# Gated cross-attention with a mixture of experts: the first query group's statistics in pairs in a written order, two products without sums first, raw key blocks read from the input

## The chip, the cores and the metric

The kernel runs on one core of one Trainium2 chip. The metric is the device time of one execution in microseconds; the median of several runs is compared. All data is float32.

## The reference

One decoder layer on 4096 tokens `x` of width 512, with a context `ctx` of 3202 rows of width 512. What matters here is the first half; `ln` is a layer norm without scale or offset.

```python
q    = ln(x)                                     # 4096 x 512
Sim  = (q @ w1)[:, None] + (ctx @ w2)[None, :] + (q * w3) @ ctx.T + b_sim
A    = softmax(Sim, axis=1)
hat  = A @ ctx                                   # 4096 x 512
Batt = softmax(max(Sim, axis=1))
bar  = Batt @ q                                  # one row
x    = x + tanh(g_xattn) * (concat[q, hat, q*hat, q*bar] @ W_qv + b_qv)
# then ln, a router over 8 experts, top 2, capacity 1280, two-layer GELU experts, scaled sum
x    = x + tanh(g_ffn) * moe(ln(x))
```

## The kernel before

The tokens are worked on in 8 groups of 512 (`g` = 0 to 7). For each group the kernel computes the scores (`stage_s`), their exponentials (`stage_e`), the weighted values (`stage_v`) and a dense product; after the last group come routing and the experts. Scores stand with context rows in partitions and tokens along the free dimension.

**The scores.** The 3202 context rows are two halves of 12 tiles of 128, one tile more, and two single rows. A key tile `j` joins tile `j` of both halves, transposed, and is worked on in pairs: six pairs a group. The 512 x 512 block of such a pair (two halves of rows, two halves of tokens, two halves of the 512 features) is computed by a Strassen-Winograd scheme: seven products of half size in place of eight, from sums of key blocks (`S1`, `S2`, `S4`, and a difference in the place of `A21`; on DVE, in `build`) and sums of query blocks (`T1`, `T2`, `T4`, and a difference in the place of `B12`; on DVE, in `right_sums`). The function `chain` issues them in the order 1, 6, 7, 5, 2, 4, 3 and joins their results on DVE (`u2`, `u3` and four sums, the score tile `E`); products 1 and 2 are summed in one PSUM bank, as are 5 and 3. Product 1 is raw keys `A11` times raw queries `B11`, product 2 is `A12` times `B21`; the others need at least one sum. One product is 8 matmul records of 128 x 256 in the profile (`pas`, `p6s`, `p7s`, `pbs`, `p4s` at L512).

**The key tiles.** In group 0, `build(j)` loads the four raw blocks of a tile from the input `ctxt_t` (512 KB, SP's queue, L361), computes the four sums (L364 to L368), and after the pair's products ACT's queue writes all seven blocks to the scratch tensor `kt_d[j]` (896 KB, L520). In groups 1 to 7 `load_keys` reads the seven blocks back (896 KB, SP's queue, L432). These tiles, and the value tiles, share a pool of five buffers (`st`), so a load waits until PE has done with the tile that had the buffer, and in group 0 also until it has been written to `kt_d`.

**The first group's queries** (`stage_a_first`) can't be prepared beside earlier work. Four tiles of 128 tokens are loaded by SP (L202). `layernorm` works tile by tile: DVE computes statistics and aggregates them (L93, L95), POOL raises the variance to the power -0.5 (L99, L100, and L101 for its square root, `sd`), DVE normalises (L102). PE transposes (L110), ACT copies from PSUM to `qT` (L205), and after each second tile the queries are scaled and shifted to `Qp` (L212 on DVE, L214 on ACT). Hints (`tc.issue_after`) order part of this: tile `t`'s statistics come after the normalising of tile `t`-2. Otherwise a planner puts each engine's instructions in order before the run; on the chip each engine follows its order and waits on semaphores.

**Constants.** ACT's queue first loads seven small constants (L57 to L165), computes `tanh` of the two gates (L69, L70; ACT loads its function table just before), and later the larger `wv` and `bqv` and the store of `qT` (L219 to L225). The column means of the router's weights `wrc` are subtracted in `stage_a_rest`, written after the third pair; the planner puts the matmuls for it (`wrps`, L253) between product 1 and product 6 of the first pair.

**Counters.** The transfers of SP's and ACT's queues share eight completion counters in turn. A transfer whose counter still belongs to an earlier transfer waits for that one to land, and what is queued behind it on its engine waits too.

Of the kernel before, what the change touches and what calls it, by code (L numbers as in the profile page):

```python
# [14 lines left out]
P = 128  # L15
# [5 lines left out]
def gated_layer(ctx, tc, x, x_t, ctxt, ctxt_t, ctxt_c, ctxt_r, g_xattn, g_ffn, w_sim, w_sim_r, b_sim, W_qv, W_qv_t, b_qv, b_qv_c, w_router, b_router, w1, b1, w2, b2, out):  # L21
# [35 lines left out]
    nc.scalar.dma_start(ws, w_sim)  # L57
# [4 lines left out]
    nc.scalar.dma_start(bsim, b_sim.partition_broadcast(P))  # L62
    gx = const.tile([P, 1], F32, name="gx")
    nc.scalar.dma_start(gx, g_xattn.partition_broadcast(P))
    gf = const.tile([P, 1], F32, name="gf")
    nc.scalar.dma_start(gf, g_ffn.partition_broadcast(P))
    bqv = const.tile([P, D], F32, name="bqv")
    tgx, tgf = gx, gf
    nc.scalar.activation(tgx, gx, AF.Tanh)  # L69
    nc.scalar.activation(tgf, gf, AF.Tanh)  # L70
# [13 lines left out]
    nc.scalar.dma_start(wrc, w_router.rearrange("(c p) e -> p c e", p=P))  # L84
    we = const.tile([P, 4, DC, E], F32, name="we")
    sd = const.tile([P, NT], F32, name="sd")

    scales, normed = [], []

    def layernorm(sm, dst, src, t):  # L90
        st = sm.tile([P, 6], F32, name=f"st{t}", tag="st")
        with tc.issue_after(normed[-2]) if len(normed) > 1 else ExitStack():
            nc.vector.bn_stats(st, src)  # L93
        mv = sm.tile([P, 2], F32, name=f"mv{t}", tag="mv")
        nc.vector.bn_aggr(mv, st)  # L95
        rstd = sm.tile([P, 1], F32, name=f"rstd{t}", tag="rstd")
        ve = sm.tile([P, 1], F32, name=f"ve{t}", tag="ve")
        with tc.issue_after(scales[-1]) if scales else ExitStack():
            nc.gpsimd.tensor_scalar(ve, mv[:, 1:2], EPS, None, ALU.add)  # L99
        scales.append(nc.gpsimd.tensor_tensor(rstd, ve, neghalf, ALU.pow).ins)  # L100
        nc.gpsimd.tensor_tensor(sd[:, t : t + 1], ve, rstd, ALU.mult)  # L101
        nrm = nc.vector.tensor_scalar(dst, src, mv[:, 0:1], rstd, ALU.subtract, ALU.mult)  # L102
        normed.append(nrm.ins)
        return nrm
# [19 lines left out]
    with ExitStack() as s1:  # L124
# [10 lines left out]
        kt_d = [dram.tile([P, 7, 2, P], F32, name=f"kt_d{j}", tag=f"kt_d{j}") for j in range(NJ)]  # L135

        kc_d = dram.tile([P, 4, 2, P], F32, name="kc_d", tag="kc_d")
        KSLOT = {"1": 0, "2": 1, "7": 2, "4": 3, "5": 4, "6": 5, "3": 6}
# [8 lines left out]
        nc.scalar.dma_start(bcol, b_qv_c)  # L147
# [17 lines left out]
        nc.scalar.dma_start(cr, ctxt_r)  # L165
# [19 lines left out]
        def right_sums(g, qT, Qp):  # L185

            B11, B12, B21, B22 = (Qp[:, r : r + 2, c : c + 256] for r in (0, 2) for c in (0, 256))
            T1, T2, T4 = (sb.tile([P, 2, 256], F32, name=f"q{k}_{g}", tag=f"qt{k}") for k in (1, 2, 4))
            tt(T1, B12, B11, ALU.subtract)
            t2 = tt(T2, B22, T1, ALU.subtract)  # L190
            tt(B12, B22, B12, ALU.subtract)
            tt(T4, B21, T2, ALU.subtract)
            live[g] = {"qT": qT, "t2": t2, "B": {"1": B11, "6": T2, "7": B12, "5": T1, "2": B21, "4": T4, "3": B22}}

        def stage_a_first():

            qT = sb.tile([P, DC, TG], F32, name="qT0", tag="qT", bufs=2)
            Qp = sb.tile([P, DC, TG], F32, name="Qp0", tag="Qp")
            qs = []
            for t in range(4):  # L200
                q = sb.tile([P, D], F32, name=f"q{t}", tag="q" if t < 3 else "mb", bufs=3 if t < 3 else 1)
                nc.sync.dma_start(q, x[t * P : (t + 1) * P, :])  # L202
                layernorm(sm, q, q, t)
                ps = transposed(ps_tr, q, f"qps{t}")
                cp = nc.scalar.copy(qT[:, :, t * P : (t + 1) * P], ps)  # L205
                qs.append(q)
                if t % 2:
                    h = slice((t - 1) * P, (t + 1) * P)
                    for c in range(DC):
                        w3, w2 = ws[:, 2 * DC + c : 2 * DC + c + 1], ws[:, DC + c : DC + c + 1]  # L210
                        if c < DC // 2:
                            qp = ts(Qp[:, c, h], qT[:, c, h], w3, w2, ALU.mult, ALU.add)  # L212
                        else:
                            live["qp"] = nc.scalar.activation(Qp[:, c, h], qT[:, c, h], AF.Identity, scale=w3, bias=w2)  # L214
                    if t == 1:
                        live["norm"] = qp
                if t == 2:
                    with tc.issue_after(cp.ins):
                        nc.scalar.dma_start(wv[:, 0, :], w_sim_r[:D].partition_broadcast(P))  # L219
                        nc.scalar.dma_start(  # L220
                            wv[:, 1:, :].rearrange("p r d -> p (r d)"), ctxt[L - NR :, :].flatten().partition_broadcast(P)
                        )
                        nc.scalar.dma_start(bqv, b_qv.partition_broadcast(P))
            right_sums(0, qT, Qp)
            nc.scalar.dma_start(qT_d[0], qT)  # L225
# [11 lines left out]
        def stage_a_rest(qs):  # L237
# [13 lines left out]
            ps = ps_tr.tile([P, DC, P], F32, name="wrps", tag="tr")[:, 0, :E]  # L251
            for c in range(DC):
                nc.tensor.matmul(ps, ones, wrc[:, c, :], start=c == 0, stop=c == DC - 1)  # L253
            mean = be
            ts(mean, ps, 1.0 / D, None, ALU.mult)
            tt(wrc, wrc, mean.unsqueeze(1).to_broadcast([P, DC, E]), ALU.subtract)
# [100 lines left out]

        def build(j):
# [1195 lines left out]
```

## Time and profile before

| | |
|---|---|
| median of 3 runs | 2637.51 us (2636.52 to 2645.64) |
| profiled execution | 2642.18 us, its span 2640.2 us |
| busy: PE, DVE, ACT, POOL | 2609.3, 1703.0, 462.6, 236.6 us |
| mean granted PE clock | 0.995 |
| moved | 436.07 MB, mean 165 GB/s |
| PE busy, 0 to 20 us and 20 to 40 us | 11.51 and 18.97 us |
| PE busy, each 20-us stretch from 100 to 1440 us | 20.00 us |

The profile is of one execution. Its times count from the start of the span; the execution's own time is 2.0 us longer than the span. PE is the matmul engine, PEld its weight loads, which overlap matmuls; ACTq and SPq are the engines' queues, in which they issue transfers. A row of the timeline has start, duration, engine, line, what is written and read, how many instructions, and in brackets how long the engine had been idle and what ended that. Because matmuls are pipelined, a row of eight lasts a little longer than the distance to the next one.

### The profile page before, as it was taken

Reading aid. Unit: us, or ns where it says so; the run is one execution under the profiler, and the core shown is the slowest. Engines: PE = TensorE matmul, PEld = TensorE weight load, DVE = VectorE, ACT = ScalarE, POOL = GpSimd, SP = SyncE. Lnnn points to the kernel's source line nnn. Section 1 sums busy time; section 2 is a strip of 40 time slices with the busy share of each in tenths; the row PEclk is TensorE's granted clock in tenths of the full one; section 3 lists DMA queues with packets and bytes.
Section 4 is the critical chain, followed back from the end, with each engine's and each line's share of the span. In section 5 each row is a group of like instructions: output and inputs, shape, how many; then the busy total and the mean of one; then the engine's idle time right before and its main releaser. Section 6 shows DMA issues by size and latency. Waiting matters only on the chain. (4 is left out here: it accounts for less than half of the span.)

```text
span 2640.2 us, 29718 instructions
## 1 busy us (share of the span) xinstructions
PE 2609.3 (99%) x11236; PEld 2104.7 (80%) x11236; DVE 1703.0 (65%) x3412; ACT 462.6 (18%) x796; POOL 236.6 (9%) x288
## 2 busy tenths in 40 slices
PE   8999999999999999999999998999999999999998
PEld 7748888888888888888888885777777777777776
DVE  7868856947768569478475566474757565565654
ACT  1201201201102002012020143212121111111111
POOL 0111000000001000000000155010101010101010
PEclk9999999999999999999999999999999999999999
DMA  8496656746747657467445794231324132223210
GB/s 316 150 290 234 207 180 192 244 149 179 255 158 196 220 162 239 159 189 245 153 144 203 279 351 162 79 124 64 128 72 145 71 128 88 104 92 100 76 60 20
DMA packets 182959, 436.07 MB, mean 165 GB/s; under 512 B 17454, under 2 KB 84270, under 8 KB 180768
## 3 DMA queue, kind: packets, MB, share of 16 engines
q1 hardware_dynamic: 150208, 352.25, 40.4%
q0 software_dynamic: 16096, 45.04, 5.0%
q10 hardware_dynamic: 16512, 36.88, 4.0%
q8 instruction: 89, 1.46, 0.2%
q14 instruction: 54, 0.44, 0.1%
HBM read 355.71 MB, written 85.55 MB: 167 GB/s over the span
## 5 line engine op out<-in xcount | busy, mean ns | idle before, releaser
L512 PE MATMUL pas<-Qp,kt 128*128 128x256 f32 x672 | 160.5, 380 | 0.0
L1299 PE MATMUL pah<-bT,w 128*128 128x320 f32 x512 | 159.3, 433 | 0.5 <-ACT p1h L1306 0.5
L662 PE MATMUL pbv<-E,vt 128*128 128x256 f32 x672 | 147.3, 379 | 0.0
L662 PEld LDWEIGHTS pbv<-E,vt 128*128 128x128 f32 x672 | 127.7, 190 | 17.4
L512 PEld LDWEIGHTS pas<-Qp,kt 128*128 128x128 f32 x672 | 127.1, 190 | 17.4 <-ACT hqT L720 0.2
L1299 PEld LDWEIGHTS pah<-bT,w 128*128 128x128 f32 x512 | 97.0, 190 | 39.7 <-ACT p1h L1306 1.0
L602 DVE TENSOR_TENSOR E<-E,mb 128x1024 f32<-128x1024 f32 x96 | 116.2, 1226 | 11.8 <-ACT mb L589 11.8
L603 ACT ACTIVATE E<-E 128x1024 f32<-128x1024 f32 x96 | 101.0, 1058 | 129.5 <-DVE E L602 128.7
L1299 PE MATMUL pao<-w,h 128*128 128x256 f32 x512 | 120.9, 379 | 0.0
L1062 PE MATMUL x1p<-W,q2T 128*128 128x264 f32 x512 | 117.5, 391 | 0.0
L1485 POOL DMA_INDIRECT out<-acc,ti x40 | 41.1, 1027 | 851.6 <-DVE acc L1484 841.8
L1462 PE MATMUL op<-w,h 128*128 128x512 f32 x256 | 114.8, 592 | 0.0
L1299 PEld LDWEIGHTS pao<-w,h 128*128 128x128 f32 x512 | 97.3, 190 | 20.1 <-issue 7.7
L1062 PEld LDWEIGHTS x1p<-W,q2T 128*128 128x128 f32 x512 | 97.8, 192 | 16.5
L468 ACT COPY p1s<-pas 128x512 f32<-128x512 f32 x48 | 28.1, 586 | 439.1 <-issue 257.0
L538 DVE TENSOR_TENSOR M<-M,E 128x1024 f32<-128x1024 f32 x80 | 98.0, 1225 | 4.3
L693 PE MATMUL vv<-E,vc 128*128 128x512 f32 x192 | 95.2, 627 | 0.0
L1462 PEld LDWEIGHTS op<-w,h 128*128 128x128 f32 x256 | 46.6, 190 | 48.7 <-issue 43.0
L1423 DVE TENSOR_TENSOR h<-p4h,u3h 128x320 f32<-128x320 f32 x64 | 31.3, 490 | 78.0 <-PE p4h L1299 76.3
L481 ACT COPY E<-pas 128x512 f32<-128x512 f32 x48 | 28.1, 586 | 303.9 <-PE pas L512 287.6
L484 DVE TENSOR_TENSOR E<-p4s,u3s 128x512 f32<-128x512 f32 x48 | 33.1, 689 | 73.5 <-PE p4s L512 73.5
L611 DVE TENSOR_TENSOR SM<-SM,E 128x1024 f32<-128x1024 f32 x64 | 78.7, 1229 | 2.5 <-ACT E L603 2.5
(449 smaller groups left out, 5470.4 us busy)
## 6 DMA issues: line engine op xcount, KB each, us to landing
kt<-kt_d SPq DMA_DIRECT2D x84, 896.0 KB
w<-in_w SPq DMA_DIRECT2D x32, 2048.0 KB
vt<-vs_d SPq DMA_DIRECT2D x56, 768.0 KB
wp<-wt_d SPq DMA_DIRECT2D x56, 520.0 KB
kt_d<-ktb ACTq DMA_DIRECT2D x12, 896.0 KB
buf_d<-zero SPq DMA_DIRECT2D x80, 129.0 KB
xb<-buf_d SPq DMA_DIRECT2D x40, 258.0 KB
r<-r_d SPq DMA_DIRECT2D x32, 260.0 KB
```

The source lines that it names most:

```text
L484: tt(done(1, 0), p4, u3, ALU.add)
L512: nc.tensor.matmul(ps[:, jl, :], kts[j][:, KSLOT[p], k, :], B[p][:, k, :], start=start and jl == 0 and k == 0, stop=stop and k == 1, skip_ ...
L538: tt(M, M, e[:, :, h], ALU.max)
L602: live[g]["last"] = tt(e, e, m, ALU.subtract)
L603: live[g]["exp"] = nc.scalar.activation(e, e, AF.Exp)
L611: tt(SM, E_t[0][:, lr] if jj == 1 else SM, E_t[jj][:, lr], ALU.add)
L662: nc.tensor.matmul(ps[b], vt[:, j - i * JH, b * P : (b + 1) * P], right(j) if j < NJ else right_c, start=start and j == 0 and b == 0, stop ...
L693: mm = nc.tensor.matmul(ps[b], vc[:, h, b * P : (b + 1) * P], E[j // 2][:, :, h, j % 2, :] if j < NJ else ec, start=j == 0 and h == 0, sto ...
L1062: mm = nc.tensor.matmul(ps[:, j, :B1], qTs[g][:, c, q * P : (q + 1) * P], W1[:, c, j, :], start=(c == 0), stop=(c == DC - 1))
L1299: nc.tensor.matmul(ps, a, b, start=start and i == 0, stop=stop and i == len(A) - 1, skip_group_check=True)
L1462: nc.tensor.matmul(ps, hT[:, k, 2 * MH :], W2[:, k, :], start=(k == 0), stop=(k == KH - 1))
L1485: sc = nc.gpsimd.indirect_dma_start(out=out[:, :], out_offset=rows_of(ti, s), in_=acc[:, :], in_offset=None, bounds_check=N - 1, oob_is_er ...
```

## The change

- `stage_a_first`: the four loads come first in SP's queue; statistics and normalising go in a written order, two tiles' statistics and aggregations, then the next two's, then four times normalising. POOL's operations take two tiles each, `sd` all four. `in_turn` chains instructions in the given order.
- ACT starts with a `tanh` of one column of ones; the constants are loaded after it (`constants`), `wrc` first.
- PE starts with five matmuls of ones (128 x 512, results unused), then computes the sums `wrps`, ahead of the transposes.
- The query halves, the key sums of the first pair and the query sums are interleaved in a written order. The subtraction of the router's means follows them.
- The first pair's chain issues 1, 2, 6, 7, 5, 4, 3, with product 2 in a PSUM bank of its own; DVE adds it to the copied product 1 (`first`).
- The input `ctxt_t` has the second half's blocks rotated, so that the three raw blocks `A11`, `A12`, `A22` are its first six 128-column blocks. `kt_d[j]` holds only the four others (512 KB). In groups 1 to 7 `load_keys` reads three blocks from the input (384 KB) and four from `kt_d` (512 KB).
- In group 0 the writes to `kt_d` are ordered after the last copy of product 2 of the pair.

The built program of the changed kernel differs from that of before, engine by engine, up to the middle of group 0, and from then on only in the 84 key loads of SP's queue, each of which has become two.

```diff
...
-        kt_d = [dram.tile([P, 7, 2, P], F32, name=f"kt_d{j}", tag=f"kt_d{j}") for j in range(NJ)]
+        kt_d = [dram.tile([P, 4, 2, P], F32, name=f"kt_d{j}", tag=f"kt_d{j}") for j in range(NJ)]
...
-        KSLOT = {"1": 0, "2": 1, "7": 2, "4": 3, "5": 4, "6": 5, "3": 6}
+        KSLOT = {"1": 0, "2": 1, "4": 2, "7": 3, "5": 4, "6": 5, "3": 6}
...
+        def constants():
+            nc.scalar.dma_start(wrc, w_router.rearrange("(c p) e -> p c e", p=P))
+            nc.scalar.dma_start(ws, w_sim)
+            nc.scalar.dma_start(gx, g_xattn.partition_broadcast(P))
+            nc.scalar.dma_start(gf, g_ffn.partition_broadcast(P))
+            nc.scalar.activation(tgx, gx, AF.Tanh)
+            nc.scalar.activation(tgf, gf, AF.Tanh)
+            nc.scalar.dma_start(bsim, b_sim.partition_broadcast(P))
+            nc.scalar.dma_start(bcol, b_qv_c)
+            nc.scalar.dma_start(cr, ctxt_r)
...
+        def in_turn(prev, ops):
+
+            for op in ops:
+                with tc.issue_after(prev.ins) if prev is not None else ExitStack():
+                    prev = op()
+            return prev
...
+            t2 = in_turn(tt(T2, B22, T1, ALU.subtract), amid)
+            with tc.issue_after(t2.ins):
+                t3 = tt(B12, B22, B12, ALU.subtract)
+            with tc.issue_after(t3.ins):
+                t4 = tt(T4, B21, T2, ALU.subtract)
...
+            junk = sm.tile([P, 1], F32, name="junk", tag="m1")
+            with tc.issue_after(nc.scalar.activation(junk, ones[:, 0:1], AF.Tanh).ins):
+                constants()
+            warm = bank("warm").rearrange("p a b -> p (a b)")
+            for _ in range(5):
+                mm = nc.tensor.matmul(warm, ones, ones.unsqueeze(1).to_broadcast([P, 4, P]), start=True, stop=True)
+
+            wr = bank("wrps")[:, 0, :E]
+            for c in range(DC):
+                with tc.issue_after(mm.ins):
+                    mm = nc.tensor.matmul(wr, ones, wrc[:, c, :], start=c == 0, stop=c == DC - 1)
...
+            keys = [load_raw(j) for j in PAIRS[0]]
...
+            for h in (0, 2):
+                st_ = [sm.tile([P, 6], F32, name=f"st{t}", tag="st") for t in (h, h + 1)]
+                last = in_turn(
+                    last,
+                    [lambda i=i: nc.vector.bn_stats(st_[i], qs[h + i]) for i in range(2)]
+                    + [lambda i=i: nc.vector.bn_aggr(mv[:, h + i, :], st_[i]) for i in range(2)],
+                )
+                with tc.issue_after(pw.ins) if pw is not None else ExitStack():
+                    nc.gpsimd.tensor_scalar(ve[:, h : h + 2], mv[:, h : h + 2, 1], EPS, None, ALU.add)
+                pw = nc.gpsimd.tensor_tensor(
+                    rstd[:, h : h + 2], ve[:, h : h + 2], neghalf.to_broadcast([P, 2]), ALU.pow
+                )
+            nc.gpsimd.tensor_tensor(sd[:, 0:4], ve, rstd, ALU.mult)
+            last = in_turn(
+                last,
+                [lambda t=t: ts(qs[t], qs[t], mv[:, t, 0:1], rstd[:, t : t + 1], ALU.subtract, ALU.mult) for t in range(4)],
+            )
+            for t in range(4):
+                with tc.issue_after(mm.ins):
+                    ps = transposed(ps_tr, qs[t], f"qps{t}")
                 cp = nc.scalar.copy(qT[:, :, t * P : (t + 1) * P], ps)
...
+            S = [key_sums(kt) for kt in keys]
+            last = in_turn(last, [lambda c=c: queries(0, c) for c in range(DC)] + S[0][:2])
+            last = in_turn(last, [lambda c=c: queries(1, c) for c in range(DC // 2)])
+            with tc.issue_after(last.ins):
+                live["sums"] = right_sums(0, qT, Qp, S[1][:2])
+            live["sums"] = in_turn(live["sums"], S[0][3:] + S[1][3:] + S[0][2:3] + S[1][2:3])
...
+        def load_raw(j):
+            kt = st.tile([P, 7, 2, P], F32, name=f"ktb{j}", tag="st")
+            with tc.issue_after(queue[-1].ins):
+                queue.append(nc.sync.dma_start(kt[:, 0:4].rearrange("p a b w -> p (a b) w"), ctxt_t[:, j, :, :]))
+            return kt
...
-            queue.append(nc.sync.dma_start(kt, kt_d[j]))
+            nc.sync.dma_start(kt[:, :3].rearrange("p a b w -> p (a b) w"), ctxt_t[:, j, :6, :])
+            queue.append(nc.sync.dma_start(kt[:, 3:], kt_d[j]))
...
+            prod(pa, "1", True, first)
+            if first:
+                p2 = bank(f"p2{name}")
+                prod(p2, "2", True, True)
...
+            if first:
+                tt(done(0, 0), p2, p1, ALU.add)
+            else:
+                prod(pa, "2", False, True)
+                live["copied"] = nc.scalar.copy(done(0, 0), pa)
...
-                        nc.scalar.dma_start(kt_d[j], kts[j])
+                        with tc.issue_after(live.get("copied", live["qp"]).ins):
+                            nc.scalar.dma_start(kt_d[j], kts[j][:, 3:])
...
-            ctxt_t[:, j, h, :, :] = rows.T.reshape(d // P, P, -1).transpose(1, 0, 2)
+            ctxt_t[:, j, h, :, :] = np.roll(rows.T.reshape(d // P, P, -1), h * (d // P // 2), 0).transpose(1, 0, 2)
```

## Prediction, made before the changed kernel had run

> **What bounds the kernel now.** I read the engine shares first, then the timeline of the first 45 us, then windows of the clock, then the waits of SP's queue.
>
> ```profile
> PE 2609.3 (99%) x11236; PEld 2104.7 (80%) x11236; DVE 1703.0 (65%) x3412; ACT 462.6 (18%) x796; POOL 236.6 (9%) x288
> ...
> kt_d<-ktb ACTq DMA_DIRECT2D x12, 896.0 KB
> ```
>
> PE is busy for all but 31 us of the span of 2640.2. In 20-us windows it is busy 20.00 of 20.00 from 100 to 1440 us: an edit there brings nothing unless it opens a hole. What the change can gain lies in the first 45 us, where the timeline shows (start, duration, engine, what, idle before and what ended it):
>
> ```profile
> 6.16 1.12 PE L110 MATMUL qps<-ident,q 128*128 128x128 f32 x4 [6.16 <-DVE q L102]
> ...
> 10.67 2.23 PE L110 MATMUL qps<-ident,q 128*128 128x128 f32 x8 [2.04 <-DVE q L102]
> ...
> 11.12 0.55 DVE L102 TENSOR_SCALAR q<-q,mv,rstd 128x512 f32<-128x512 f32 x1 [0.60 <-POOL rstd L100]
> ...
> 12.70 3.62 PE L512 MATMUL pas<-Qp,ktb 128*128 128x256 f32 x8
> ...
> 16.11 1.40 PE L253 MATMUL wrps<-wrc,ones 128*128 128x8 f32 x8
> ...
> 17.37 1.97 PE L512 MATMUL p6s<-q,ktb 128*128 128x256 f32 x8
> ...
> 27.81 1.89 PE L512 MATMUL pas<-Qp,ktb 128*128 128x256 f32 x8
> ...
> 34.48 0.43 DVE L364 TENSOR_TENSOR ktb<-ktb 128x256 f32<-128x256 f32 x1 [4.45 <-DMA ktb<-in_ctxt_t]
> ...
> 39.36 1.99 PE L512 MATMUL pbs<-Qp,ktb 128*128 128x256 f32 x8 [1.03 <-DVE E L479]
> ```
>
> Four losses stand there. PE starts the first product at 12.70, because the last query tile is normalised only at 11.67. That product takes 3.62 us where a later one takes 1.89: its records are (3.62-0.635)/7 = 0.43 us apart, later ones (29.54-27.81)/8 = 0.216, so PE runs at half speed. The router sums (wrps) stand between products 1 and 6 and take 17.37-16.11 = 1.26. And at 39.36 PE lost 1.03 us (1.1 with the restart): a key tile landed only at 34.4, DVE stood still for it, and its later additions came late.
>
> **What the skill says.** "TensorE: Matmul & The Clock Gate", What's actually happening: the array starts at half clock and changes by how busy a free-running window of 3413 ns was. The trace agrees, though the page's clock row shows full speed in the first slices. Columns here: busy time and count per engine, then clock, DMA share, GB/s.
>
> ```profile
> 97.00:99.00 2.00, 1.76 (x12) 1.43 (x12) 1.51 (x6) 0.00 (x0) 0.28 (x1) 0.99 0.87 330
> 99.00:101.00 2.00, 2.00 (x10) 1.49 (x8) 0.55 (x1) 0.59 (x1) 0.10 (x1) 0.50 0.07 25
> 109.00:111.00 2.00, 2.00 (x9) 1.28 (x8) 2.00 (x3) 0.00 (x0) 2.00 (x1) 0.95 0.00 0
> ...
> 1631.00:1635.00 4.00, 3.25 (x15) 2.81 (x16) 0.69 (x1) 0.88 (x2) 0.00 (x0) 0.57 1.03 335
> ```
>
> The clock falls at 98.96 and rises at 109.20: 28.99 and 31.99 windows of 3.413 from the span's start. On that grid the first rise is at 17.07, in the middle of wrps, as its records show (1.40 us for eight, against 1.04 at full speed near 95 and 1.7 at half). The page's Part 4 says that transposes don't count as busy in the same way; here they do: from 1631.75 only transposes ran, and the clock rose after 3.44 us. "DMA: Bandwidth & Descriptors", Anatomy of one DMA, gives 2.0 us of fixed cost per transfer (for GpSimd's queue); I use it as an upper estimate for each additional key transfer. "Trainium Kernel Development and Optimization", Key Constraints: all queues share 16 DMA engines. The trace agrees: while ACT's kt_d writes of 896 KB drain (18 to 32 us, DMA share about 1.0), the key tile that SP issued at 27.14 took 7.3 us to land.
>
> **The change, step by step**, on the grid of this execution.
>
> *Statistics (DVE, POOL).* Tile 1 arrives at 4.77 as before, its statistics end at 5.46, two aggregations at 5.79. From an aggregation's end to the normalise it feeds before took 5.59-4.48 = 1.11 us through POOL, so pair one is ready at 6.9. But the fixed order first runs tiles 2 and 3: two statistics 1.53, two aggregations 0.30, to 7.54. The fourth load had waited 1.6 us for a counter and no longer does; I estimate its arrival at 5.3 to 6.3, ahead of its use at 6.6. Normalising: tile 0 at 8.06 (later than before's 6.10), tile 1 at 8.6, tile 2 not before 7.54+1.11 = 8.65, so 9.2, tile 3 at 9.7. Before 11.67: 2.0 us won on DVE. POOL loses seven small operations, which were hidden but for those waits.
>
> *Warm-up and wrps (PE).* Ten records of 512 columns, 0.85 each at half and 0.43 at full speed (twice the 256-column spacing), from 1.1. With the rise at 6.83, 6.7 of them are through, and the rest end at 8.25; wrps, eight at 0.116 (1.04 us row), ends at 9.2. It needs wrc, whose load ACT now issues only after the table load and a small tanh (1.28+0.20 from 0.75), at about 2.3. With the 3 us that the first loads take, it is there by 6. SP's load of the second key tile is queued behind that counter; it is needed at 12. The tile 0 transpose, ready at 8.1, waits to 9.2.
>
> *Transposes and queries.* At full speed four transpose records take 0.66 (the mps row at 95.95); ACT's copies 0.59, alternating over two banks: last copy from 11.8 to 12.4 (before 13.73). Query halves on DVE: four, 0.34 apart, from 11.1 to 12.5; ACT's two end at 13.5.
>
> *Products.* Product 1 needs raw keys and two query blocks: 11.6 to 13.35. Product 2 is raw too: to 15.05. On DVE follow two sums of tile 0 (13.4), two query blocks (14.1), T1 and T2 (0.8 apart, 15.64), two sums of tile 1 (16.5), two more query sums (17.8), the first sum of product 7 (18.2). So product 6 starts at 15.7 (hole 0.65), product 7 at 18.25 (hole 0.8), and 7, 5, 4, 3 end at 18.25+4x1.727 = 25.15. Before, the next chain began at 27.81: **-2.65**. ACT's copy of product 1 is queued behind four DMA issues (13.5 to 15.2) and is wanted only after product 6, at 17.4; wrps's bank is freed near 19.5, and product 4 takes it at 21.7.
>
> *Second hole.* kt_d writes shrink to 512 KB, and are issued near 19.5. The key tile wanted next is issued when product 3 frees its buffer (24.3), finds the engines nearly free, and lands near 27.5; DVE reaches it near 31. The hole of **-1.1** goes. What is late next: DVE's addition before the last product of that pair, done at 34.8, wanted at 35.5. That cover is thin.
>
> *Groups 1 to 7.* 84 loads of 896 KB become 84 of 384 and 84 of 512. SP's additional issues: 84x0.32 = 27 us over 1240, beside waits that look like this:
>
> ```profile
> SPq L432 <- PE pbs L512: 257.2, 41, 13.0
> ```
>
> SP waits for PE to free buffers, not PE for SP. The tile issued at 380.82 had landed at 384.7 (3.9 us), and is first used near 392.7: 8 us of slack for 0.32 plus at most 2.0. So 0; the cover is the five-buffer pool. The rest of group 0 starts 3.75 earlier and is otherwise the same; the half-speed stretch from 98.96 can shift by a fraction of a window, about 1 us either way.
>
> **Sum**: -2.65-1.1 = -3.75, with ends -5 (clock rises at 3.41, transposes start at 8.1) and -0.8 (below). The profiled execution took 2642.18 and would take 2638.4; it lies 4.7 above the median of the runs, so the median 2637.5 goes to 2633.8.
>
> **Rivals.**
> 1. *The clock doesn't rise in time.* The warm-up then only stands in front of the transposes: 10 records at half speed to 9.6, wrps to 11.35, last transpose done at 15.1. Product 1 from there, rise at 17.07, product 3 ends at 28.15, 0.35 later than before; with the hole gone -0.75: 2636.8. For it: the window's phase is free; about 3.4 us between warm-up and product 1 hold only small work. Against: transposes counted at 1631.
> 2. *Slower: split key loads run late.* It decides once a tile takes over 392.7-380.8 = 11.9 us to land, against 3.9 now. If each of 42 pairs were late by 0.3, +12.6-3.75: 2646.4. For it: twice as many transfers share eight completion counters. Against: SP's waits.
> 3. *More than computed*: DVE's sums interleave without the holes at products 6 and 7 and the transposes start early, another -2.5: 2631.
>
> **Numbers.** Forecast 0.75, rival 1 0.14, rival 2 0.05, rival 3 0.06. About 0.5%, 13.2 us, is what a measurement of this kernel can tell from no change, and the whole prologue holds less than that: faster by more 0.02, within 0.96, slower by more 0.02. The range 2629 to 2641 takes in the forecast's ends, rivals 1 and 3 and the scatter of the runs (2636.5 to 2645.6), and leaves out rival 2.
>
> **What would show it.** Right: product 1 near 11.6 with 1.9 us, wrps ahead of the transposes, the second pair's first product near 25, no wait for ktb near 34, PE 20.00 of 20.00 from 100 to 1440. Wrong: 128x512 records at 0.85 to the end of the warm-up, product 1 with 3.6 us, or any PE wait for kt in groups 1 to 7.

## The result, and the profile after

Measured beside the kernel before on the same chip, the changed kernel takes 2633.89 us (median of 14 runs, 2629.81 to 2637.09) against 2637.09 us (14 runs). The ratio is 0.9984, with a 95% interval from 0.9977 to 0.9991: 4.2 us less, between 2.4 and 6.1. Measured again on another chip it was 0.9978 (0.9968 to 0.9988), 5.8 us less. The ratio is not that of the two medians, which differ by 3.2 us. Both gains are well under the 0.5% that the prediction took for the least that a measurement of this kernel can tell; "no change" lies outside both intervals all the same. The predicted 2633.8 us lies at the median.

The two profiled executions differ by more, 2642.18 against 2632.46 us. Half of that is not the change, as the last section shows. What the change did is read at fixed places of the program: where certain products start in each trace.

The timeline of PE in the changed kernel, first 27 us (start, duration, engine, what, idle before and what ended it):

```profile
1.07 6.28 PE L200 MATMUL warm<-ones 128*128 128x512 f32 x10 [1.07 <-DVE ones L52]
7.18 0.95 PE L205 MATMUL wrps<-wrc,ones 128*128 128x8 f32 x8
...
10.46 1.08 PE L85 MATMUL qps<-ident,q 128*128 128x128 f32 x8 [0.59 <-DVE q L232]
11.38 1.89 PE L563 MATMUL pas<-Qp,ktb 128*128 128x256 f32 x8
13.12 1.89 PE L563 MATMUL p2s<-Qp,ktb 128*128 128x256 f32 x8
15.08 1.99 PE L563 MATMUL p6s<-q,ktb 128*128 128x256 f32 x8
17.41 1.99 PE L563 MATMUL p7s<-Qp,ktb 128*128 128x256 f32 x8 [0.34 <-DVE ktb L406]
...
26.15 1.89 PE L563 MATMUL p6s<-q,ktb 128*128 128x256 f32 x8
```

Product 1 starts at 11.38 (before 12.70) and takes 1.89 us (before 3.62). `wrps` stands ahead of the transposes, and `p2s` follows product 1 without a gap. Products 6 and 7 still wait: 15.08 is 0.23 us later than 13.12 plus one product of 1.727, and 17.41 is 0.60 us later than 15.08 plus one product (0.34 of it stands in brackets; the rows' modelled ends hide the rest). The second pair's products 1 and 2 are now interleaved with the last of the first pair, so I count its start as that of its product 6 less 1.727: 26.15 - 1.73 = 24.42, before 27.81.

The timeline of DVE in the same stretch:

```profile
6.75 1.31 DVE L221 BATCH_NORM_STATS2 st<-q 128x6 f32<-128x512 f32 x2 [1.47 <-DMA q<-in_x]
...
9.77 1.00 DVE L232 TENSOR_SCALAR q<-q,mv,rs 128x512 f32<-128x512 f32 x2 [0.61 <-POOL rs L226]
```

The 1.47 us ahead of 6.75 are new: the third query tile is late, and everything behind that wait on DVE moves with it. (In a second profile of the same kernel it is the fourth tile that is late; E5 shows it.) The row at 9.77 is the normalising of the third and fourth tile, to 10.77.

For groups 1 to 7, from the page: the engine line and the two transfer lines of the key tiles (count, size, median us to landing); and from the waits, SP's queue waiting for buffers (us in total, times, longest):

```profile
PE 2609.6 (99%) x11246; PEld 2103.0 (80%) x11246; DVE 1702.3 (65%) x3415; ACT 460.8 (18%) x794; POOL 225.3 (9%) x281
...
kt<-kt_d SPq DMA_DIRECT2D x84, 512.0 KB, 4.6
...
kt<-in_ctxt_t SPq DMA_DIRECT2D x84, 384.0 KB, 6.0
```

```profile
SPq L478 <- PE pbs L563: 238.3, 28, 12.5
```

PE's busy time is as before (2609.3 us there). SP still waits for PE to free buffers, with 238.3 us in total a little less than before (257.2), and PE's list of waits from 200 to 1440 us is empty. The two parts of a key tile take 6.0 and 4.6 us to land in the median, inside the 11.9 us at which the prediction put the limit.

### The profile page after: what moved, and what is told of

Its sections match the earlier page's. It is cut to its first block, busy times and chain, and to the rows that moved or that the text cites. A ratio compares the mean times of both kernels' runs of the same rounds, so it can differ in the third digit from the quotient of the medians.

```text
span 2630.7 us, 29857 instructions
## 1 busy us (share of the span) xinstructions
PE 2609.6 (99%) x11246; PEld 2103.0 (80%) x11246; DVE 1702.3 (65%) x3415; ACT 460.8 (18%) x794; POOL 225.3 (9%) x281
## 5 line engine op out<-in xcount | busy, mean ns | idle before, releaser
L658 DVE TENSOR_TENSOR E<-E,mb 128x1024 f32<-128x1024 f32 x96 | 115.1, 1215 | 12.4 <-ACT mb L645 12.4
L1355 PE MATMUL p6h<-x,w1s 128*128 128x320 f32 x256 | 79.6, 433 | 0.0
L563 PE MATMUL pbs<-Qp,kt 128*128 128x256 f32 x336 | 79.5, 379 | 0.0
```

The lines of the kernel that those rows point to most:

```text
L563: nc.tensor.matmul(ps[:, jl, :], kts[j][:, KSLOT[p], k, :], B[p][:, k, :], start=start and jl == 0 and k == 0, stop=stop and k == 1, skip_ ...
L658: live[g]["last"] = tt(e, e, m, ALU.subtract)
L1355: nc.tensor.matmul(ps, a, b, start=start and i == 0, stop=stop and i == len(A) - 1, skip_group_check=True)
```

## The experiments

All are read at four places: the start of product 1, the start of the second pair, the scores of the one unpaired tile of context rows that follows group 0's six pairs (`sc`), and the first product of group 1. From the second pair to `sc` five pairs take 61.6 us if PE never waits; the column "waits" is what a trace has above that. "Again" is the changed kernel in a second profile. E3 to E7, and E5 and E7 together in this table, are one execution each, so their whole times aren't compared.

| kernel | product 1 | second pair | waits | `sc` | group 1 |
|---|---|---|---|---|---|
| before | 12.70 | 27.81 | 1.5 | 90.93 | 201.50 |
| changed | 11.38 | 24.42 | 0.0 | 86.02 | 196.53 |
| changed, again | 11.43 | 24.66 | 0.0 | 86.26 | 195.61 |
| E1 without the third part | 11.02 | 24.06 | 2.4 | 88.09 | 196.97 |
| E2 third part alone | 12.77 | 27.34 | 0.2 | 89.16 | 198.21 |
| E3 no warm-up | 12.92 | 25.73 | 0.0 | 87.33 | 196.08 |
| E4 order 1, 6, 7 | 11.57 | 26.33 | 0.0 | 87.93 | 197.10 |
| E5 keys held | 10.69 | 23.73 | 0.0 | 85.32 | 195.89 |
| E6 tile by tile | 11.27 | 24.31 | 0.0 | 85.91 | 194.67 |
| E7 5 before 6 | 11.72 | 23.81 | 0.1 | 85.50 | 196.06 |
| E5 and E7 together | 10.59 | 23.00 | 0.1 | 84.69 | 193.45 |

The changed kernel's two profiles agree to 0.24 us up to `sc`. But where product 1 starts depends on when the last query tile lands, and that changes from execution to execution: the five profiles whose program is the same up to there (changed, again, E1, E4, E7) have product 1 from 11.02 to 11.72. So a difference of half a microsecond in a start, from one profile, may be no more than that. Distances are steadier: from product 1 to the second pair it is 13.04 us in the changed kernel, E1 and E6, and 13.23 in the second profile. The last column isn't steady either; why is told at the end.

### E1: the change without its third part

The third part of the change is the last in the title: three raw key blocks are read from the input, so that only four blocks, 512 KB, are written to `kt_d` and read back.

```diff
-        kt_d = [dram.tile([P, 4, 2, P], F32, ...) for j in range(NJ)]
+        kt_d = [dram.tile([P, 7, 2, P], F32, ...) for j in range(NJ)]
-            nc.sync.dma_start(kt[:, :3].rearrange("p a b w -> p (a b) w"), ctxt_t[:, j, :6, :])
-            queue.append(nc.sync.dma_start(kt[:, 3:], kt_d[j]))
+            queue.append(nc.sync.dma_start(kt, kt_d[j]))
-                            nc.scalar.dma_start(kt_d[j], kts[j][:, 3:])
+                            nc.scalar.dma_start(kt_d[j], kts[j])
```

> The change without its third part: the scratch tensor keeps seven blocks (896 KB a tile), groups 1 to 7 load a key tile in one transfer. Theory A (two independent gains: the first pair worth 3.4 us, and a further 1.3 us at the third pair because the smaller writes free the DMA engines for a key tile that was late): the second pair's first product starts near 24.4 as in the full change, then a wait of PE for DVE of 1.0 to 1.3 us comes back between the second and third pair, so the first group of group 1 starts near 197.8 (before 201.50, full change 196.53). Theory B (the earlier, different order of the prologue alone removes that wait, the size of the writes has nothing to do with it): no such wait, group 1 starts at 196.5. Groups 1 to 7 take 1255.8 us in both cases; were the split loads what costs, this kernel would be shorter there than the full change. Time against before: A -3.7 us (0.9986), B -5.0 us (0.9981).

The second pair starts at 24.06, as both theories have it. Between the second and the third pair nothing waits, which is theory B; but waits come back all the same, 2.4 us, at the sixth pair. The timelines of DVE, at the third pair's tile and at the sixth's, and of PE at the sixth pair:

```profile
29.24 0.43 DVE L403 TENSOR_TENSOR ktb<-ktb 128x256 f32<-128x256 f32 x1 [0.59 <-DMA ktb<-in_ctxt_t]
```

```profile
71.94 0.42 DVE L403 TENSOR_TENSOR ktb<-ktb 128x256 f32<-128x256 f32 x1 [2.25 <-DMA ktb<-in_ctxt_t]
```

```profile
78.06 1.99 PE L562 MATMUL pbs<-Qp,ktb 128*128 128x256 f32 x8 [0.96 <-DVE E L529]
```

The key tile that landed at 34.4 in the kernel before is there at 29.2 here, with the large writes: the new order of the prologue is enough for that one. Later the writes of 896 KB meet 4 MB of loads for `wq`: SP issues these from 49.13 to 64.66 (48.55 to 60.21 in the changed kernel) and the sixth pair's first key tile behind them, at 65.96 (60.33). That tile comes 2.25 us too late for DVE, which passes it on to PE. So the third part seems to remove waits, but not in the place where the prediction saw them. This wait is from one profile; none of the ten with small writes has more than 0.2 us. Time against before: 0.9994 (0.9985 to 1.0002), where `sc` is 2.84 us earlier: the interval takes in no change, so E1's gain is shown by the trace alone.

### E2: the third part alone

```diff
-        kt_d = [dram.tile([P, 7, 2, P], F32, ...) for j in range(NJ)]
+        kt_d = [dram.tile([P, 4, 2, P], F32, ...) for j in range(NJ)]
-            A11, A12, A21, A22, S1, S2, S4 = (kt[:, k, :, :] for k in range(7))
+            A11, A12, A22, A21, S1, S2, S4 = (kt[:, k, :, :] for k in range(7))
-            queue.append(nc.sync.dma_start(kt, kt_d[j]))
+            nc.sync.dma_start(kt[:, :3].rearrange("p a b w -> p (a b) w"), ctxt_t[:, j, :6, :])
+            queue.append(nc.sync.dma_start(kt[:, 3:], kt_d[j]))
-                        nc.scalar.dma_start(kt_d[j], kts[j])
+                        nc.scalar.dma_start(kt_d[j], kts[j][:, 3:])
```

The input is rotated and `KSLOT` reordered as in the full change.

> The kernel before with the third part alone: raw blocks read from the rotated input, 512 KB a tile to and from the scratch tensor, two loads a tile in groups 1 to 7. Theory A: nothing changes to the second pair (product 1 at 12.70 with 3.62 us, second pair at 27.81), and the wait of 1.03 us at 39.36 goes, with the 0.23 us one at 68.8: group 1 starts near 200.2 (before 201.50). Theory B (that wait hangs on the prologue): it stays, 201.5. Groups 1 to 7 take 1255.8 us by both; a cost of the second load would show there as more than 1256. Time against before: A -1.3 us (0.9995), B 0.

Theory A holds for the wait at 39.36. DVE at the third pair's first tile, and PE at the product that waited at 39.36 before:

```profile
30.11 0.43 DVE L364 TENSOR_TENSOR ktb<-ktb 128x256 f32<-128x256 f32 x1 [0.55 <-DMA ktb<-in_ctxt_t]
```

```profile
37.70 1.89 PE L513 MATMUL pbs<-Qp,ktb 128*128 128x256 f32 x8
```

The tile lands at 30.1, 4.4 us earlier than before, and PE's row has no idle time in brackets where before stood 1.03 us. The 0.23 us wait near 68 stayed. The second pair starts 0.47 us earlier than before only because the clock rose before `wrps` instead of during it (0.95 us for its row, 1.40 before). Time against before: 0.9992 (0.9985 to 0.9998), `sc` 1.77 us earlier. E1 and E2 add up to 4.6 us at `sc`; the full change has 4.91.

E1 and E2 together say: either the new prologue or the small writes alone removes the wait at the third pair. That the sixth pair needs the small writes once the prologue is faster rests on E1's one profile.

### E3: no warm-up

```diff
-            warm = bank("warm").rearrange("p a b -> p (a b)")
-            for _ in range(5):
-                mm = nc.tensor.matmul(warm, ones, ones.unsqueeze(1).to_broadcast([P, 4, P]), start=True, stop=True)
...
```

> The full change without the five warm-up matmuls (whose results nobody uses); the router sums still come first on PE. Theory A (the warm-up raises the clock, and that is worth the second half of product 1 and more): product 1 takes about 3.6 us, the clock rises one or two windows of 3.4 us later, at 13.7 to 17.1, and the second pair starts 0.5 to 3.5 us later than the 24.4 of the full change. Theory B (DVE's sums are what bounds the first pair; the waits of PE ahead of products 6 and 7, 0.23 and 0.6 us, and DVE's order swallow a slower product 1): second pair at 24.4 to 25.0. Theory C (the transposes raise the clock by themselves): product 1 takes 1.9 us all the same and nothing moves.

DVE at the fourth query tile, and PE's timeline:

```profile
7.97 0.69 DVE L218 BATCH_NORM_STATS2 st<-q 128x6 f32<-128x512 f32 x1 [1.89 <-DMA q<-in_x]
```

```profile
9.37 3.76 PE L85 MATMUL qps<-ident,q 128*128 128x128 f32 x16 [2.64 <-DVE q L229]
12.92 2.43 PE L560 MATMUL pas<-Qp,ktb 128*128 128x256 f32 x8
15.19 1.89 PE L560 MATMUL p2s<-Qp,ktb 128*128 128x256 f32 x8
16.92 1.89 PE L560 MATMUL p6s<-q,ktb 128*128 128x256 f32 x8
```

Theory A has the direction: the second pair starts 1.31 us later. But not all of that is the warm-up's. In this execution the fourth query tile came late (7.97), and the last normalising ended at 11.38, 0.61 us later than in the changed kernel (10.77). What is left for the missing warm-up is 0.70 us: from the last normalising to the second pair it is 14.35 us here, 13.65 in the changed kernel's first profile. In its second, where the clock rose late, it is 14.08, and only 0.27 is left.

Product 1 starts at 12.92, 1.54 us after the last normalising in place of 0.61, because 16 transpose records run at half speed, and its first 2.5 records still do ((15.19 - 12.92 - 1.727)/0.216), so the clock rises near 14.0. The expected 3.6 us for product 1 were too many: the transposes before it already count as activity, as theory C has it, only too late. The waits ahead of products 6 and 7 are gone (16.92 = 15.19 + 1.73; product 7 is 0.07 late): they can have absorbed part of what the half clock cost.

### E4: the first pair in the old order

```diff
-                e_add = chain(f"s{g}_{jj}", prod, lambda i, j: e[:, j, i, :, :], g == 0 and jj == 0)
+                e_add = chain(f"s{g}_{jj}", prod, lambda i, j: e[:, j, i, :, :])
```

> The full change with the first pair's chain in the order of before (1, 6, 7, 5, 2, 4, 3, products 1 and 2 in one bank); DVE's written order of sums stays. Theory A (product 2 fills the time in which DVE makes the sums for 6 and 7): product 6 still waits for T2 until about 15.1, PE stands still for 1.9 to 2.2 us after product 1, and the second pair starts 1.7 us later, at 26.1. Theory B (PE would have the sums early enough, since 6 waits only for its own): product 6 starts before 14, second pair at 24.4 to 24.8.

PE's timeline:

```profile
11.57 1.89 PE L563 MATMUL pas<-Qp,ktb 128*128 128x256 f32 x8
15.26 1.99 PE L563 MATMUL p6s<-q,ktb 128*128 128x256 f32 x8 [1.80 <-DVE q L182]
```

Product 6 starts at 15.26, when DVE has made `T2`, whatever stands before it. Without product 2 there, PE waits 1.96 us after product 1 (15.26 - 11.57 - 1.73) and the second pair starts at 26.33, 1.91 us later; counted from product 1, which started 0.19 us later here, it is 14.76 us in place of 13.04. Theory A: placing product 2 second is worth 1.72 us, one product.

### E5: the first pair's key loads held back

```diff
-            keys = [load_raw(j) for j in PAIRS[0]]
+            keys = [load_raw(j, qs[3]) for j in PAIRS[0]]
...
+            if behind is not None:
+                nc.scalar.copy(kt[:, 0, 0, 0:1], behind[:, 0:1])
```

> The full change, with the first pair's two key loads held back until the fourth query tile has landed (ACT copies one column of that tile into each key buffer ahead of its load, which the load then overwrites). In the full change DVE stood still for 1.47 us (5.28 to 6.75) for the third query tile, though its load had been issued at 1.67. Theory A (that tile was late because the key tile's load, issued at 2.62, shares the 16 DMA engines with it): third and fourth tile land by 5.3 to 5.8, the fourth is normalised near 9.3 to 9.6 in place of 10.8, product 1 starts near 10.4 (11.38 in the full change), and the second pair near 23.5 to 24.0 (24.42), less only if the key tiles, about 1.5 us later, are now late for product 1 or for DVE's sums. Theory B (the query tiles take so long by themselves, 5.1 us from issue to landing): third tile at 6.7 as before, product 1 at 11.3 or later.

DVE's statistics of the third and fourth tile, then product 1 and its weight loads (PEld):

```profile
5.37 0.69 DVE L221 BATCH_NORM_STATS2 st<-q 128x6 f32<-128x512 f32 x1
6.67 0.69 DVE L221 BATCH_NORM_STATS2 st<-q 128x6 f32<-128x512 f32 x1 [0.60 <-DMA q<-in_x]
```

```profile
10.69 2.20 PE L565 MATMUL pas<-Qp,ktb 128*128 128x256 f32 x8
...
11.75 0.73 PEld L565 LDWEIGHTS pas<-Qp,ktb 128*128 128x128 f32 x4 [0.44 <-DMA ktb<-in_ctxt_t]
```

The same statistics of the fourth tile in the changed kernel's second profile:

```profile
7.18 0.69 DVE L221 BATCH_NORM_STATS2 st<-q 128x6 f32<-128x512 f32 x1 [0.93 <-DMA q<-in_x]
```

Theory A holds in kind, but for another tile than the one that it names. DVE takes the third tile at 5.37 here and at 6.75 in the changed kernel's first profile. In its second profile, though, with nothing held, it takes it at 5.55 (E1 5.46, E3 5.39, E4 5.49, E7 5.29): the late third tile was a matter of that one execution. What the held loads change in every profile is the fourth tile. Its statistics begin at 6.58 to 6.69 in the three profiles with held key loads (this one and the two of both edits below), and at 7.01 to 7.97 in six without (changed, again, E1, E3, E4, E7). So the key tile's load, issued at 2.62, after the query tiles' four, does slow the last of them. By how much it is in one execution can't be said: without the hold that tile alone spreads over 1 us.

Product 1 starts 0.69 us earlier, short of the 1.0 expected; the three held profiles have it at 10.59 to 10.94, the six with a warm-up and nothing held at 11.02 to 11.72. It takes 2.03 us to the next product in place of 1.73, since PE's weight loads wait 0.44 us for a key tile, as the expectation allowed for. The second pair gains 0.69 us all the same: the 0.3 us take up the 0.23 that product 6 would have waited for DVE's sums.

### E6: statistics tile by tile

```diff
-                    [lambda i=i: nc.vector.bn_stats(st_[i], qs[h + i]) for i in range(2)]
-                    + [lambda i=i: nc.vector.bn_aggr(mv[:, h + i, :], st_[i]) for i in range(2)],
...
+                for i in (h, h + 1):
+                    last = in_turn(last, [lambda: nc.vector.bn_stats(st_, qs[i]), lambda: nc.vector.bn_aggr(mv[:, i, :], st_)])
...
+                    [lambda t=t: ts(qs[t], qs[t], mv[:, t, 0:1], rstd[:, t : t + 1], ALU.subtract, ALU.mult) for t in (h, h + 1)],
```

> The full change with the statistics taken tile by tile on DVE and POOL, and tiles 0 and 1 normalised before the statistics of tiles 2 and 3, as the order of before had it; loads, warm-up and products stay. Theory A (the pairing is worth the 2.0 us that the prediction put down to it): the fourth tile is normalised at 12 or later, product 1 starts at 12.5 to 13, the second pair at 25.5 or later. Theory B (what counts is that the loads no longer wait, and that the warm-up ends before the first transpose; DVE waits for the third tile anyway, and has the time for two normalisings in that wait): product 1 starts at 11.1 to 11.7, the second pair at 24.2 to 24.7.

DVE normalises the second tile and then takes the third's statistics:

```profile
6.57 0.55 DVE L226 TENSOR_SCALAR q<-q,mv,rs 128x512 f32<-128x512 f32 x1 [0.47 <-POOL rs L223]
7.19 0.70 DVE L220 BATCH_NORM_STATS2 st<-q 128x6 f32<-128x512 f32 x1
```

Theory B: product 1 at 11.27, the second pair at 24.31, both 0.11 us earlier than in the changed kernel, which is less than two executions of one program can differ by. While the later tiles are still on their way, this order normalises two. So pairing tiles is worth nothing as long as the tiles land this late; with the key loads held it wasn't tried.

### E7: product 5 ahead of product 6

```diff
-            last = in_turn(last, [lambda c=c: queries(0, c) for c in range(DC)] + S[0][:2])
+            last = in_turn(last, [lambda c=c: queries(0, c) for c in range(DC)] + S[0][:1] + S[1][:1])
-                live["sums"] = right_sums(0, qT, Qp, S[1][:2])
+                live["sums"] = right_sums(0, qT, Qp, S[0][1:2] + S[1][1:2])
...
                 p2 = bank(f"p2{name}")
                 prod(p2, "2", True, True)
+                pb = bank(f"pb{name}")
+                prod(pb, "5", True, False)
...
```

> The full change with the first pair's chain in the order 1, 2, 5, 6, 7, 4, 3, and DVE's sums in the order that it needs (T1 directly after the four first query halves and the two key sums, T2, then the first tile's second key sum and so on). Theory A (what stood ahead of products 6 and 7 was DVE's chain of sums, 0.23 and 0.6 us, and product 5, which needs only one query sum and one key sum, can run earlier and give DVE 1.7 us more): both waits go, the second pair starts at 23.5 to 23.7 (24.42 in the full change). Theory B (DVE is short in sum, not in order: the wait moves to product 5 or 4): second pair at 24.2 or later.

PE's timeline from product 5 to product 7:

```profile
15.18 1.89 PE L566 MATMUL pbs<-q,ktb 128*128 128x256 f32 x8
16.90 1.89 PE L566 MATMUL p6s<-q,ktb 128*128 128x256 f32 x8
18.63 1.89 PE L566 MATMUL p7s<-Qp,ktb 128*128 128x256 f32 x8
```

Theory A: each starts 1.73 us after the one before; no wait is left. The second pair gains 0.61 us although product 1 started 0.34 us later in this execution (the fourth query tile came at 7.71). Counted from product 1 it gains 0.95 us, 12.09 in place of 13.04: the two waits of 0.23 and 0.60 us and the 0.10 that PE lost at product 5.

### Both together, and the changed kernel once more

> The last two edits that are meant to gain, together: the first pair's key loads held until the query tiles have landed, and product 5 ahead of product 6. If both theories A hold and add, the second pair starts near 22.7 to 23.2 (24.42 in the full change, 27.81 before), 1.2 to 1.7 us earlier than the full change. If the earlier transposes only move the wait to DVE's sums, which then bound, it starts no earlier than with the better of the two alone.

The two edits add: the second pair starts 1.42 us earlier than in the changed kernel's first profile, `sc` 1.33 us earlier. Timed next to the changed kernel:

> The full change with the key loads held and product 5 ahead of product 6, timed beside the full change. Its second pair started 1.4 us and its first scores 1.3 us earlier in the profile; everything after is the same. Theory A: 1.4 us faster than the full change, 5.5 to 6.3 us faster than before (0.9976 to 0.9979), with an interval that likely can't tell it from the full change. Theory B (the gain is given back later in group 0): as the full change.

It took 2633.34 us (6 runs) where the changed kernel took 2633.53 us (9 runs) and the kernel before 2638.65 us. Against before that is 0.9970 (0.9958 to 0.9982), and for the changed kernel 0.9978 (0.9968 to 0.9988): a lower estimate, but the intervals overlap, so whether it beats the changed kernel as a whole is not shown. In this second profile the early start was there (`sc` at 84.93), and 1.5 us went later, in groups 1 to 7. DVE and PE in group 2, where the worst of it stands:

```profile
418.58 0.69 DVE L352 BATCH_NORM_STATS2 st<-q 128x6 f32<-128x512 f32 x1 [2.81 <-DMA q<-in_x]
```

```profile
419.98 1.89 PE L568 MATMUL p4s<-q,kt 128*128 128x256 f32 x8
422.40 1.78 PE L568 MATMUL pbs<-Qp,kt 128*128 128x256 f32 x7 [0.53 <-DVE E L535]
```

DVE stood still for 2.81 us for a query tile of the next group, whose load SP issues among key loads; the sums behind it came late, and PE waited 0.53 us by the list, 0.69 with the restart (422.40 - 419.98 - 1.73). Such waits reached PE in three of the ten profiles with split key loads (E2, E5 and this one; groups 1 to 7 are 1.2 to 1.5 us longer in each, in E5 partly by a late value tile) and in neither of the two without (before, E1). These three are also the profiles in which DVE's longest wait for such a tile was 2.5 to 2.8 us; in the other nine it was 0.55 (before) to 1.78 us (E1) and reached PE in none. That is too few profiles to charge it to the split loads.

> The changed kernel once more. Theory A (the clock's windows have a free phase, so a profile's times differ by it): up to the first scores (86.02 in the first profile) times agree within 0.3 us, but the half-speed stretch of group 0, which lasted from about 93.7 to 103.4, starts or ends elsewhere, and the way from the first scores to the first product of group 1, 110.51 us there, is 108.8 to 110.6, by 0, 1 or 2 windows. Theory B (the kernel's own order sets it): 110.5 again. Time against before 0.998 (first measurement 0.9984, 0.9977 to 0.9991).

Theory A holds: up to `sc` the two profiles agree to 0.24 us, and from `sc` to group 1 they take 110.51 and 109.35 us. Windows of 2 us in the first profile and in the second (busy time and count per engine, then granted clock, DMA share, GB/s):

```profile
93.00:95.00 2.00, 1.76 (x4) 0.91 (x4) 0.68 (x4) 0.00 (x0) 0.38 (x1) 0.58 0.52 198
...
103.00:105.00 2.00, 2.00 (x6) 1.09 (x7) 2.00 (x3) 2.00 (x4) 1.33 (x1) 0.86 0.03 8
```

```profile
95.00:97.00 2.00, 2.00 (x14) 2.00 (x13) 1.57 (x2) 0.71 (x2) 0.00 (x0) 0.65 0.12 45
...
103.00:105.00 2.00, 2.00 (x9) 1.09 (x8) 2.00 (x3) 2.00 (x3) 1.33 (x1) 1.00 0.00 0
```

In the first, the clock is half from about 93.3 (0.58 in the window) to 103.6 (0.86): three of the clock's windows of 3.41 us. In the second it is half from about 95.6 (0.65) to before 103: two. The same code, the same work.

## Why the prediction was right, and where it was not

**The sum.** Predicted -3.75 us; at `sc` the traces show -4.91 and -4.67. That the median came within 0.1 us of the predicted one is luck: the measured gain is only known to lie between 2.4 and 6.1 us, and several terms of the sum were wrong in both directions. The profiled execution was to take 2638.4 us; the two took 2632.46 and 2636.69, and the clock's scatter, which the range allowed for, is larger than what is missing in the sum. The prologue was undersized (-2.65 predicted, -3.39 and -3.15 at the second pair), the second hole a little too (-1.1 predicted, -1.5 of waits gone).

**Statistics: the size and the reason failed.** The fourth tile was to be normalised at 9.7; it is at 10.77 (9.77 + 1.00) in the first profile and 10.58 in the second, so 0.9 to 1.1 us were won on DVE and not 2.0. Two terms failed. One is the estimated arrival of the last load at 5.3 to 6.3: DVE waited for the third tile until 6.75 in the first profile and for the fourth until 7.18 in the second, so that the aggregations end at 8.28 (8.09) in place of 7.54. I had counted only the wait for a counter, and not that a key tile's load issued next shares the engines; E5 shows that this costs the fourth tile time. The other is POOL:

```profile
8.87 0.87 POOL L226 TENSOR_TENSOR rs<-ve,neghalf 128x2 f32<-128x2 f32 x1
```

From the aggregations' end to the normalising, two tiles at once took 1.49 us (8.28 to 9.77), where 1.11, one tile's time, had been put in. And the gain that there is doesn't come from pairing (E6: 0.11 us the other way). What remains of this part is that the loads no longer wait for a counter, as the fourth query tile's did before (SP's queue, us in total, times, longest):

```profile
SPq L202 <- DMA ws<-in_w_sim: 1.6, 1, 1.6
```

That wasn't tested by itself. That there are eight counters, used in turn, is to be seen in the changed kernel: the ninth transfer of the two queues, the load of `gf`, is issued at 3.40, just when the first, the first query tile, has landed and DVE reads it (3.56 and 3.56 in the second profile).

**Warm-up and `wrps`: right in kind, but the clock is worth less.** With the warm-up the clock had risen before the transposes in all nine profiles that have it: its ten records took 6.00 to 7.42 us, and would have taken 8.5 at half speed throughout. It rose near 4.6 in the first profile, where the warm-up's weight loads go from 0.85 to 0.43 us apart, and near 6.9 in the second, whose warm-up row is 1.14 us longer (7.42). The predicted 6.83 came from a grid that I tied to the span's start, which was a coincidence of one profile. In the second profile the transposes did wait for `wrps`, to 9.13 (predicted 9.2), and product 1 came 0.85 us after the last normalising, not 0.61; that it started at 11.43, next to 11.38, is because the last query tile was 0.19 us earlier. Rival 1 put 3.0 us on the clock (product 3 ends at 28.15 in place of 25.15); E3, which has no warm-up at all and whose difference of 1.31 us holds 0.61 of a late query tile, shows 0.3 to 0.7 in its one execution, since there the clock rose near 14.0 and not at 17.07. The load of `wrc` was issued at 1.05, not 2.3, while ACT's table load (0.75 to 2.03) still ran.

**Transposes and queries: the time is right, by luck.** The last copy ended at 12.20 (11.8 to 12.4), DVE's query halves 0.34 us apart. But the prediction let the transposes begin at 9.2, behind `wrps`, and had the last tile ready at 9.7. They began at 8.76, and the last tile was ready 1.07 us late; the two errors cancelled.

**Products: right in kind, too dear.** The two holes were there, at the named products and from the named sums, at 0.23 and 0.60 us where 0.65 and 0.8 were computed. DVE had `T2` at 15.02 (computed 15.64), having begun the query halves at 10.69 and not at 11.1. E4 and E7 confirm what holds these products: DVE's sums in the order written.

**Second hole: right in size, half right in its cause.** The wait near 39 went. But smaller writes were not needed for it (E1), though they are enough (E2); by E1's one profile they were needed for a later place that the prediction didn't name. The "thin cover" held in all profiles.

**Groups 1 to 7: right.** From the first product of group 1 to the first dense product after group 7: 1457.26 - 201.50 = 1255.76 us before, 1452.30 - 196.53 = 1255.77 after. Rival 2 is refuted for key tiles; if split loads cost anything, then through the query tiles, in some executions.

**Rivals.** Rival 1 (clock) is refuted in all nine profiles with the warm-up. Rival 3 (more than computed) holds in part: smaller holes, 0.9 to 1.2 us more in place of 2.5.

## What to carry to other kernels

Read a small change at fixed places of the program, not at the end: the whole time needed 14 runs to show four microseconds. Then look at what comes ahead of such a place. Product 1 started up to 0.7 us apart in profiles of the same prologue, because a query tile landed earlier or later, and 0.61 of E3's 1.31 us were no more than that; distances from one place to the next were steadier. A load that is issued later can still delay the one before it, so hold back what isn't wanted yet. And when an engine waits for sums, put first whatever product needs none: here, where the wait was longer than a product, it was worth its whole length (E4), as long as the sums follow in the order in which they are wanted (E7).

## What the hardware showed that I had not expected

- The clock's windows have their own phase. The Trainium skill ("TensorE: Matmul & The Clock Gate", What's actually happening) calls the window free-running, and the runs agree. By the granted clock from 91 to 115 us, the half-speed stretch in group 0 lasts one window of 3.4 us in three of the twelve profiles, two in four and three in five, and the way from `sc` to group 1 follows it in all twelve: 108.75 to 108.76 us with one window (E3, E6, both), 108.88 to 109.35 with two (again, E1, E2, E4), 110.14 to 110.57 with three (before, changed, E5, E7, both in the second profile). So up to 1.8 us in the table's last column are the phase of the window, and its order is not that of `sc`.
- The granted clock goes with much of the scatter of whole runs. Over the 14 runs of the changed kernel the time falls with the mean granted clock, from 2635.6 to 2637.1 us at 0.994 to 2629.8 us at 0.998 (correlation -0.92; -0.59 over the 33 runs of the kernel before that were timed beside E1). And of the 9.5 us by which the two profiled spans differ, 4.96 stand at the end of group 7; the rest arises after that, in code that the change doesn't touch.
- Transposes count as activity for the clock: in E3 the 3.4 us before the rise near 14.0 held transposes to 12.9 and only then product 1. In the profile before, a stretch of transposes alone had raised it.
